# dt and u*dt spread over the partitions through DRAM tiles, so that a state-space scan reads both operands from SBUF

## The chip, the cores and the metric

One NeuronCore of one Trainium2 chip. The metric is the device time of one execution in microseconds (us), the median over runs. Everything is float32.

## The reference

The input is x of shape (2, 2048, 256). Two feed-forward steps stand around a state-space block, each with a residual (layer norms without parameters):

```
x = x + 0.5 * ffn(layernorm(x))      # 8 groups of 512 tokens, W1 (1024x256), W2 (256x1024), no nonlinearity between
x = x + ssm(layernorm(x))
x = x + 0.5 * ffn(layernorm(x))

def ssm(x):                          # 512 inner channels, 16 states each
    x_in, z = split(x @ Wi.T + bi)
    u  = silu(causal depthwise conv of 4 taps over x_in + conv_b)
    dt = softplus(x_in[..., :32] @ Wdt.T + bdt)
    h_t = h_(t-1) * exp(dt_t * A) + dt_t * Bm * u_t          # for every channel and state
    y_t = sum over states of h_t * Cm
    return (y * silu(z)) @ Wo.T + bo + x * Dv.mean()
```

The recurrence over t is the heart: 512 channels x 16 states x 4096 time steps.

## The kernel before, in words

The 4096 tokens go through in four blocks of 1024 (`s` = 0 to 3; blocks 0 and 1 are one sequence, 2 and 3 the other, so the scan state is carried from an even block to the odd one behind it). The 512 channels are cut in eight units of 64 (`j`), two of them to a quarter `q`. For one unit a tile of 128 partitions holds 64 channels x 2 halves of 512 tokens; two of the 32 units, those of quarter 0 in block 0 and quarter 3 in block 3, are laid out otherwise ("wide": 128 channels x 512 tokens, so a scan falls into two of 512 elements).

A scan works on 32 channels x 4 states = 128 partitions and 1024 tokens at once. So each unit takes eight scans: two halves `a` of its channels x four groups `m` of states, in the order that `ORDER` lists. The kernel counts these in one running position `t` from 0 to 255 (8 positions a unit, 64 a block), and all other work is hung on positions.

For a scan (line 691, VectorE, `tensor_tensor_scan`: g = dec * g + v along the tokens) two operands are made:

- `dec` = exp(dt * -A), one ScalarE activation (line 678) from `rep`. `rep` is dt of 32 channels, repeated on the four groups of 32 partitions, by eight DMAs of 64 KB from SBUF to SBUF for each (unit, half) (`spread_dt`, line 646, SyncE's queue). `dec` has four SBUF buffers.
- `v` = u * dt, made by GpSimd (line 630, into a tile `v`) and spread over the partitions by TensorE (`spread_v`, line 662): matmuls with a 0/1 matrix `sel_rep` put it in a PSUM tile of two banks (pool `ps_v`, two buffers, four of the eight PSUM banks). So a scan reads `dec` from SBUF and `v` from PSUM. B and C are folded together into the weights `wy`, which are made once for all 64 columns.

After a scan GpSimd copies its last column to `state` in even blocks (line 693), and TensorE sums over the states (line 700): 16 matmuls (`py`) for each pair of scans, into one PSUM bank (pool `ps_y`, one buffer). ScalarE copies the finished `py` to SBUF (line 707) and GpSimd multiplies it with the gate z (line 711). Everything else in PSUM shares three banks (pool `ps`).

Beside the scans run the preparation of later quarters (`Prepare`: projections on TensorE line 488, the convolution's taps on GpSimd lines 529 and 530, softplus on ScalarE line 94, v on GpSimd line 630), the output projection of the block before (line 732), its second feed-forward step and the first one of the next block (`Ffn`, `Second`: layer-norm sums on VectorE line 322, additions on GpSimd lines 395, 414, 447, 451, 741), and the products W1 W2 of later groups on TensorE (line 259). The first feed-forward step of block 0 and the first operands stand ahead of the loop and are written out by hand.

The order on every engine's queue is the order of the program: nothing reorders it (`manual_schedule`). A table `PL` of positions says at which `t`, counted from the block's or the quarter's start, each step is issued; at one position steps go by kind, those of TensorE behind the others. ScalarE, VectorE, GpSimd and SyncE's DMA queue are in order too, so a step that waits holds up what stands behind it on its own engine. The exponential of scan t is issued three positions ahead (`LA`).

Of the kernel before, what the change touches and what calls it, by code (L numbers as in the profile page):

```python
# [74 lines left out]
def macaron_kernel(ctx: ExitStack, tc: tile.TileContext, x, wi_t, wo_t, wdt_t, par, w1, w2_t, b1, b2, bo, out):  # L75
# [10 lines left out]
    p5 = ctx.enter_context(tc.tile_pool(name="p5", bufs=5))  # L86
    p8 = ctx.enter_context(tc.tile_pool(name="p8", bufs=8))
    ps_y = ctx.enter_context(tc.tile_pool(name="ps_y", bufs=1, space=bass.MemoryType.PSUM))
    ps_v = ctx.enter_context(tc.tile_pool(name="ps_v", bufs=2, space=bass.MemoryType.PSUM))
    ps = ctx.enter_context(tc.tile_pool(name="ps", bufs=3, space=bass.MemoryType.PSUM))  # L90
# [18 lines left out]
    def load_w(g, k, pool=None):  # L109

        w1v = w1[g].rearrange("(p oc) h -> p oc h", p=P)
        w2v = w2_t[g].rearrange("(p oc) h -> p oc h", p=P)
        if pool is None:
            a = wpool.tile([P, NO // 2, DM], F32, tag="w1", name=f"w1_{g}_{k}")
            b = wpool.tile([P, NO // 2, DM], F32, tag="w2", name=f"w2_{g}_{k}")
        else:
            a, b = (
                pool.tile([P, TB], F32, tag="g", name=f"w{i}_{g}_{k}").rearrange("p (a b) -> p a b", b=DM)
                for i in (1, 2)
            )  # L120
        nc.sync.dma_start(a, w1v[:, k * NO // 2 : (k + 1) * NO // 2, :])
        nc.sync.dma_start(b, w2v[:, k * NO // 2 : (k + 1) * NO // 2, :])
        w_sb[g, k] = (a, b)
# [19 lines left out]
    load_w(0, 0)  # L143
    S.dma_start(b1_sb, b1.rearrange("p g o -> p (g o)"))
    load_x(0, 1, S)
    load_w(0, 1)
    for k in range(2):
        load_w(1, k, p5)
    nc.sync.dma_start(wi_sb, wi_t.rearrange("(hh p) d -> p hh d", p=P))

# [44 lines left out]

    early = p2.tile([P, CH], F32, tag="ev", name="early")
    sel32 = early[:, NPAIR * 2 * NM :][:, :32]
    sel_rep = const.tile([P, 2, P], F32, name="sel_rep")
    GP.memset(sel_rep, 0.0)
# [3 lines left out]
    cb_g = early[:, : NPAIR * 2 * NM].rearrange("p (a b) -> p a b", b=1)  # L203
    wy = const.tile([P, NPAIR * 2 * NM, 32], F32, name="wy")
    dv_mean = const.tile([P, 1], F32, name="dv_mean")

    def make_sel_rep():
# [3 lines left out]
        for p in range(4):  # L211
            r = slice(p * 32, (p + 1) * 32)
            GP.tensor_copy(sel_rep[r, p % 2, :].rearrange("p (b c) -> p b c", b=4),
                           sel32[r, :].rearrange("p (b c) -> p b c", b=1).to_broadcast((32, 4, 32)))
# [15 lines left out]
    def make_wy(lo, hi):  # L230
        n = hi - lo
        GP.tensor_tensor(
            wy[:, lo:hi, :], sel32.rearrange("p (a b) -> p a b", a=1).to_broadcast((P, n, 32)),
            cb_g[:, lo:hi, :].to_broadcast((P, n, 32)), ALU.mult,
        )
# [226 lines left out]
    class Prepare:  # L462
# [102 lines left out]
        def exp_table(self, tables=LN_EXP):  # L565
            S.preload_act_table_set(tables)
# [29 lines left out]
        def silu(self):  # L596
            S.activation(self.u, self.u, AF.Silu)  # L597
            self.silu_zs()
# [7 lines left out]
        def start_v(self):  # L606
            v_sb[self.s, self.q] = p1.tile([P, NJ2, CH], F32, tag="v", name=f"v_{self.n}")

        def half_dve(self, u):

            if u == 0:
                self.start_v()
            V.scalar_tensor_tensor(v_sb[self.s, self.q][:, u, :], self.u[:, u, :], 0.5, dts[self.s, self.unit(u)],
                                   ALU.mult, ALU.mult)

        def drive_dve(self, u):
            v = v_sb[self.s, self.q][:, u, :]
            V.scalar_tensor_tensor(v, self.th[:, u, :], 1.0, v, ALU.add, ALU.mult)

        def drive_gp(self, u):  # L620
            if u == 0:
                self.start_v()
            GP.tensor_scalar(self.th[:, u, :], self.th[:, u, :], 0.5, 0.5, ALU.mult, ALU.add)
            GP.tensor_tensor(self.u[:, u, :], self.u[:, u, :], self.th[:, u, :], ALU.mult)
            GP.tensor_tensor(v_sb[self.s, self.q][:, u, :], self.u[:, u, :], dts[self.s, self.unit(u)], ALU.mult)

        def drive(self, eng, u):
            if u == 0:
                self.start_v()
            eng.tensor_tensor(v_sb[self.s, self.q][:, u, :], self.u[:, u, :], dts[self.s, self.unit(u)], ALU.mult)  # L630
# [5 lines left out]
    def column(s, j, a, c, m):  # L636

        group = (j // NJ2) * 4 + (a * 2 + c if is_wide(s, j) else (j % NJ2) * 2 + a)
        return group * NM + m

# [8 lines left out]
    def spread_dt_pe(s, j, a):  # L649

        reps[s, j, a] = []
        for c in range(2):
            t = ps_y.tile([P, CH], F32, tag="py", name=f"pr_{c}") if c else bank(f"pr_{c}")
            r = rows(is_wide(s, j), a, c)
            T.matmul(t, lhsT=sel_rep[r, r.start // 32 % 2, :], rhs=dts[s, j][r, :], start=True, stop=True)
            reps[s, j, a].append(t)

    def spread_v(s, j, a):
        t = ps_v.tile([P, TB], F32, tag="v", name=f"pv_{s}_{j}_{a}")
        for c in range(2):  # L660
            r = rows(True, a, c) if is_wide(s, j) else slice(c * HC, (c + 1) * HC)
            T.matmul(t[:, c * CH : (c + 1) * CH], lhsT=sel_rep[r, c if is_wide(s, j) else a, :],  # L662
                     rhs=v_sb[s, j // NJ2][r, j % NJ2, :], start=True, stop=True)
# [8 lines left out]
    def exponential(t):  # L672
        s, j, a, m = place_of(t)
        decs[t] = p4.tile([P, TB], F32, tag="dec", name=f"dec_{t}")
# [20 lines left out]
    def output(s, j, m):  # L695
        if m == 0:
            pys[s, j] = ps_y.tile([P, CH], F32, tag="py", name=f"py_{s}_{j}")
        for c in range(2):
            for a in range(2):
                T.matmul(pys[s, j][rows(is_wide(s, j), a, c), :], lhsT=wy[:, column(s, j, a, c, m), :],  # L700
# [70 lines left out]
    def fill(n):  # L771

        for _ in range(n):
            T.matmul(next(reversed(pys.values()))[:31, :P], lhsT=b1_pad[:, 0, 1:], rhs=sel_rep[:, 0, :], start=False, stop=False)
# [3 lines left out]
    busy(12)  # L778
    settle(first[0])
    turn(first[0])  # L780
    for hh in range(2):
        combine(0, 0, hh)
    settle(first[1])
    pad_bias(0)
    load_par()
    make_sel_rep()
    bias_pe(0, (0,))
# [3 lines left out]
    bias_pe(0, (1,))  # L791
    bias_act(0)
# [29 lines left out]
    begin.exp_table(EXP)  # L822
# [12 lines left out]
    make_wy(0, 16)  # L835
# [9 lines left out]
    PL = {'g0': 8, 'g1': 11, 'si': 12, 'po0': 3, 'po1': 7, 'poa': 4, 'c0': 12, 'c1': 28, 'f3a': 13, 'f3b': 17, 'f1a': 20, 'f1b': 30, 'sa': 32, 'sb': 41, 'nw': 0, 'nr': 2, 'tp0': 3, 'ta0': 5, 'tp1': 4, 'ta1': 6, 'bi': 7, 'pr0': 7, 'pr1': 8, 'ad0': 9, 'ad1': 10, 'rs': 3, 'rb': 7, 'i0': 0, 'i1': 0, 'ia': 2, 'ed': 2, 'ce': 3, 'tp': 5, 'dr': 12, 'dv0': 4, 'dv1': 7, 'cb': 8, 'bp': 2, 'ba': 5, 'sp': 8, 'sq': 9, 'lw': 6, 'lx0': 16, 'lx1': 28, 'st': 12, 'r0': 0, 'r1': 4, 'xg0': 2, 'xs0': 5, 'xf0': 7, 'xf1': 16, 'xg1': 8, 'xs1': 14, 'xw': 23, 'xp0': 12, 'xp1': 29, 'xd': 18, 'xr0': 29, 'xb0': 35, 'xr1': 32, 'xb1': 40, 'y0': 11, 'y1': 12, 'y2': 13, 'y3': 17, 'y4': 16, 'y5': 18, 'z0': 6, 'z1': 8, 'z2': 8, 'z3': 10, 'ga': 2, 'gm': 2, 'eo': 3, 'en': 4, 'ep': 6, 'eb': 8, 'u0': 1, 'u1': 1, 'u2': 1, 'u3': 2, 'u4': 3, 'u5': 4, 'u6': 5, 'u7': 5, 'u8': 6, 'u9': 7, 'ua': 11}  # L845
    plan = {}

    def at(t, fn, *a, name=None):
# [4 lines left out]
        if t % 1:  # L853
            kind = 4
# [9 lines left out]
    def put_ffn(t, s, h, name):  # L864
        put(t, lambda: Ffn(s, h, name), (0, "stats"), (PL["nw"], "newton", GP), (PL["nr"], "normalise", 0, GP),
            (PL["nr"], "normalise", 1, GP), (PL["tp0"], "turn_pe", 0), (PL["ta0"], "turn_act", 0),
            (PL["tp1"], "turn_pe", 1), (PL["ta1"], "turn_act", 1), (PL["bi"], "bias", GP), (PL["pr0"], "product", 0),
            (PL["pr1"], "product", 1), (PL["ad0"], "add_act", 0), (PL["ad0"], "add_gp", 0),
            (PL["ad1"], "add_act", 1), (PL["ad1"], "add_gp", 1))

    def put_second(t, s, h):
        put(t, lambda: Second(s, h), (0, "stats"), (PL["nw"], "newton", GP), (PL["nr"], "normalise", 0, GP),
            (PL["nr"], "normalise", 1, GP), (PL["tp0"], "turn_pe", 0), (PL["ta0"], "turn_act", 0),
            (PL["tp1"], "turn_pe", 1), (PL["ta1"], "turn_act", 1), (PL["rs"], "residual"), (PL["rb"], "residual_bias"))

    def put_prepare(t, s, q):
        if (s, q) == (0, 1):
# [3 lines left out]
                (PL["z3"], "drive_gp", 0),  # L881
# [3 lines left out]
        steps = [(PL["i0"], "inner_pe", 0), (PL["i1"], "inner_pe", 1), (PL["ia"], "start_xi"), (PL["ia"], "inner_act", 0),  # L885
                 (PL["ia"], "inner_act", 1), (PL["ed"], "edges"), (PL["ce"], "centre", 0), (PL["ce"], "centre", 1)]
        steps += [(PL["tp"] + n, "tap", k, i)
                  for n, (k, i) in enumerate((k, i) for k in (2, 1, 0) for i in range(NJ2))]
        steps += [(PL["g0"], "gate_pe", 0), (PL["g1"], "gate_pe", 1), (PL["si"], "silu"),
                  (PL["dr"], "drive", GP, 0), (PL["dr"], "drive", GP, 1)]  # L890
        if q == 0:
            for j in range(NPAIR):
                d = PL["dv0"] if j < NPAIR // 2 else PL["dv1"]
                steps += [(d, "dt_pe", j), (d, "dt_act", j)] + ([(d, "exp_table")] if j % 4 == 3 else [])
        put(t, lambda: Prepare(s, q), *steps)
# [3 lines left out]
    for t, method, *a in (  # L899
# [7 lines left out]
        (PL["u6"], begin.dt_pe, 1), (PL["u6"], begin.dt_act, 1), (PL["u6"], begin.exp_table, EXP),  # L907
# [4 lines left out]
        (PL["ua"] + 0.5, begin.exp_table, EXP),  # L912
        (PL["xg1"], begin.gate_pe, 1), (PL["xs1"], begin.gate_z, 1), (PL["xs1"], begin.gate_z_times, 1),
        (13, make_wy, 16, 32), (PL["xw"], make_wy, 32, 64),
# [6 lines left out]
    for s in range(NB):  # L921
        b = s * PER
        for j in range(NPAIR):
            t = b + j * NPOS
            nxt = (s, j + 1) if j + 1 < NPAIR else (s + 1, 0)
            if nxt[0] < NB:
                for k in range(2):
                    at({(0, 1): 6, (0, 2): 10}.get(nxt, t + PL[f"r{k}"]), spread_dt, *nxt, k)
# [3 lines left out]
        for q in range(NQ):  # L932
            if q + 1 < NQ:
                put_prepare(b + q * 2 * NPOS, s, q + 1)
            elif s + 1 < NB:
                put_prepare(b + q * 2 * NPOS, s + 1, 0)
# [152 lines left out]
```

## Time and profile before

| | |
|---|---|
| median of two runs | 767.4 us (766.62 and 768.19) |
| the profiled execution | 764.32 us, span in the trace 762.5 us |
| granted TensorE clock in it, mean | 0.937 |
| busy, share of the span: TensorE | 642.3 us, 84% |
| VectorE | 638.6 us, 84%, of it the scans 574.4 us |
| ScalarE | 527.1 us, 69%, of it the exponentials dec 292.4 us |
| GpSimd | 512.9 us, 67% |
| DMA of SyncE's queue | 59.84 MB, 28.9% of 16 DMA engines |

Busy time is time in which an instruction ran; the idle time of an engine is listed with what ended it (its releaser). The first scan starts at 42.2 us and the last ends about 744 us, so the span falls into a head of 42 us, the scans with all that runs beside them, and a tail of 18.5 us.

### The profile page before, as it was taken

What the parts mean: (1) busy time and instruction counts of PE and PEld (TensorE: products, weight loads), DVE (VectorE), ACT (ScalarE), POOL (GpSimd) and SP (SyncE); (2) the same over time, 40 slices, a digit from 0 to 9 for tenths busy, and PEclk for the clock granted to TensorE, in tenths of its full rate; (3) what the DMA queues carried; (4) which work ended last, traced back from release to release, by engine and by line L of the source; (5) the groups of instructions that cost most, each with busy time, mean ns of one, the idle gap of its engine ahead of it and who ended that gap; (6) DMA issues with size and microseconds to landing.
All of it is one profiled execution on the core that took longest, in us unless ns stands there. A gap on an engine that the chain in (4) does not pass through costs nothing.

```text
span 762.5 us, 10406 instructions
## 1 busy us (share of the span) xinstructions
PE 642.3 (84%) x3428; PEld 277.1 (36%) x3428; DVE 638.6 (84%) x553; ACT 527.1 (69%) x658; POOL 512.9 (67%) x821
## 2 busy tenths in 40 slices
PE   9999795993879998897888998897697989677966
PEld 7634241440212543542211643353121524212534
DVE  3587777793999989776999989776999999999995
ACT  3467885753899576765899675757699777768631
POOL 5125658899854759979853779989964678753321
PEclk9999799997899999999899999999799999897989
DMA  8274216242122325415122325313122222322101
GB/s 298 72 220 113 55 29 166 56 125 68 28 56 65 74 56 155 135 38 160 40 55 56 73 67 142 112 51 75 37 56 55 56 57 75 92 56 55 29 1 55
DMA packets 42789, 62.29 MB, mean 82 GB/s; under 512 B 12536, under 2 KB 22128, under 8 KB 42736
## 3 DMA queue, kind: packets, MB, share of 16 engines
q1 hardware_dynamic: 41344, 59.84, 28.9%
q0 software_dynamic: 720, 1.24, 0.6%
q8 instruction: 27, 0.44, 0.2%
q10 hardware_dynamic: 672, 0.56, 0.2%
q14 instruction: 26, 0.21, 0.1%
HBM read 24.08 MB, written 4.19 MB: 37 GB/s over the span
## 4 chain that ended last, share of the span: by engine, by line
PE 39%; POOL 22%; DVE 13%; ACT 11%; issue 6%; DMA 6%; SPq 2%; ACTq 0%; DVEq 0%; POOLq 0%
DVE g L691 11%; PE pwc L259 7%; PE py L700 7%; PE po L732 7%; POOL u L530 5%; ACT dec L678 5%; PE pv L662 4%; DMA rep<-dt 3%; PE pf_f L402 3%; PE pxi L488 3%; POOL tap L529 3%; DMA w<-in_w_t 2%; POOL x L414 2%; POOL x L395 2%; PE pz L488 2%
## 5 line engine op out<-in xcount | busy, mean ns | idle before, releaser
L678 ACT ACTIVATE dec<-rep,neg_a 128x1024 f32<-128x1024 f32 (+1 forms) x280 | 287.6, 1059 | 122.4 <-DVE g L691 82.9
L691 DVE TENSOR_TENSOR_SCAN g<-dec,state,pv 128x1024 f32<-128x1024 f32 (+1 forms) x160 | 309.5, 2003 | 26.6 <-PE py L700 13.0
L691 DVE TENSOR_TENSOR_SCAN g<-dec,pv 128x1024 f32<-128x1024 f32 (+1 forms) x128 | 264.9, 2131 | 34.4 <-PE py L700 17.2
L700 PE MATMUL py<-g,wy 128*32 128x512 f32 x1024 | 167.7, 654 | 51.1 <-ACT ev_y L707 35.0
L530 POOL TENSOR_TENSOR u<-u,tap 128x512 f32<-128x512 f32 x90 | 114.2, 1268 | 9.0 <-ACT u L524 1.6
L662 PE MATMUL pv<-v,sel_rep 64*128 64x512 f32 (+1 forms) x256 | 72.8, 663 | 31.9 <-POOL v L630 15.2
L693 POOL COPY state<-g 128x1 f32<-128x1 f32 x160 | 27.5, 185 | 80.0 <-DVE g L691 80.0
L700 PEld LDWEIGHTS py<-g,wy 128*32 128x32 f32 x1024 | 25.2, 111 | 147.4 <-issue 60.6
L711 POOL TENSOR_TENSOR z<-ev_y,z 128x512 f32<-128x512 f32 x31 | 39.6, 1276 | 50.3 <-ACT ev_y L707 50.3
L402 PE MATMUL pf_f<-wc,xnt_f 128*128 128x256 f32 x256 | 66.5, 405 | 5.9 <-ACT ev_f L410 4.3
L529 POOL TENSOR_SCALAR tap<-xi,par_p 128x512 f32<-128x512 f32 x84 | 58.1, 692 | 8.7 <-DMA xi<-xi 5.4
L488 PE MATMUL pz<-xn2t,wi_sb 128*64 128x512 f32 x224 | 61.9, 681 | 0.0
L259 PE MATMUL pwc<-w,w 128*128 128x256 f32 x256 | 60.8, 386 | 0.2 <-ACT dt L94 0.2
L402 PEld LDWEIGHTS pf_f<-wc,xnt_f 128*128 128x128 f32 x256 | 48.0, 197 | 32.5 <-ACT ev_f L410 8.2
L732 PE MATMUL po<-wo_sb,z 64*128 64x256 f32 x448 | 54.6, 391 | 0.8 <-POOL z L711 0.7
L259 PEld LDWEIGHTS pwc<-w,w 128*128 128x128 f32 x256 | 47.1, 190 | 18.4 <-issue 8.9
L488 PE MATMUL pxi<-xn2t,wi_sb 128*64 128x512 f32 x224 | 51.1, 598 | 0.0
L732 PEld LDWEIGHTS po<-wo_sb,z 64*128 64x128 f32 x448 | 43.5, 192 | 16.8 <-issue 10.6
L395 POOL TENSOR_TENSOR x<-x,bc 128x1024 f32<-128x1024 f32 x14 | 33.0, 2355 | 23.4 <-ACT xn_f L361 23.4
L662 PEld LDWEIGHTS pv<-v,sel_rep 64*128 64x128 f32 (+1 forms) x256 | 19.6, 190 | 75.6 <-DVE g L691 35.3
L630 POOL TENSOR_TENSOR v<-u,dt 128x512 f32<-128x512 f32 x28 | 35.0, 1270 | 6.9 <-ACT u L597 6.9
L414 POOL TENSOR_TENSOR x<-ev_f,x 128x512 f32<-128x512 f32 x24 | 30.4, 1269 | 3.1 <-ACT ev_f L410 3.1
(158 smaller groups left out, 745.1 us busy)
## 6 DMA issues: line engine op xcount, KB each, us to landing
rep<-dt SPq DMA_DIRECT2D x496, 64.0 KB, 2.0
w<-in_w SPq DMA_DIRECT2D x16, 512.0 KB, 6.9
w<-in_w_t SPq DMA_DIRECT2D x16, 512.0 KB, 8.7
x<-in_x SPq DMA_DIRECT2D x7, 512.0 KB, 3.9
out<-x SPq DMA_DIRECT2D x6, 512.0 KB, 3.2
wi_sb<-in_wi_t SPq DMA_DIRECT2D x1, 1024.0 KB, 13.8
wo_sb<-in_wo_t SPq DMA_DIRECT2D x2, 512.0 KB, 6.7
out<-x SPq DMA_DIRECT2D x4, 256.0 KB, 2.2
```

Source lines behind the costliest of these rows:

```text
L259: T.matmul(pt, lhsT=a[:, oc, hh * P : (hh + 1) * P], rhs=b[:, oc, :], start=(k == 0 and oc == 0), stop=(k == 1 and oc == NO // 2 - 1),)
L395: eng.tensor_tensor(self.xs, self.xs, bc[self.g].to_broadcast((P, GT, DM)), ALU.add)
L402: T.matmul(o, lhsT=self.xt[pair][:, hh, k * P : (k + 1) * P], rhs=wc[self.g][:, hh, :], start=(hh == 0), stop=(hh == NH - 1 and not bias))
L414: GP.tensor_tensor(part, self.ev.rearrange("p (a b) -> p a b", a=2), part, ALU.add)
L488: T.matmul(pt[h * HC : (h + 1) * HC, :], lhsT=wi_sb[:, hh, k : k + HC], rhs=xn2t[self.s, h][:, hh, :], start=(hh == 0), stop=(hh == NH - 1))
L529: GP.tensor_scalar(tap, self.xi[:, u, k : k + CH], self.par(C_CW, NK, u, k), 0.0, ALU.mult, ALU.add)
L530: GP.tensor_tensor(self.u[:, u, :], self.u[:, u, :], tap, ALU.add)
L662: T.matmul(t[:, c * CH : (c + 1) * CH], lhsT=sel_rep[r, c if is_wide(s, j) else a, :], rhs=v_sb[s, j // NJ2][r, j % NJ2, :], start=True, s ...
L678: S.activation(decs[t][:, c * w : (c + 1) * w], part, AF.Exp, scale=neg_a[:, i : i + 1])
L691: V.tensor_tensor_scan(g[:, r], dec[:, r], v[:, r], 0.0 if first else state[:, i : i + 1], ALU.mult, ALU.add)
L700: T.matmul(pys[s, j][rows(is_wide(s, j), a, c), :], lhsT=wy[:, column(s, j, a, c, m), :], rhs=gs[a, m][:, c * CH : (c + 1) * CH], start=(m ...
L732: T.matmul(held_po[s, pair][h][:, k * DM : (k + 1) * DM], lhsT=lhsT, rhs=rhs, start=((q, i) == parts[0]), stop=((q, i) == parts[-1]))
```

## The change

- `dt` and `v` of each unit are written to DRAM tiles of 128 x 512 by one DMA (`to_dram`) and read back into SBUF four times, once for each group of 32 partitions (`from_dram`: four DMAs of 128 KB for each half, for dt into `rep`, for v into a new tile `vr` with three buffers). All go through SyncE's queue. Units 0 and 1 of block 0 keep the old ways: `spread_dt`, and `spread_v` by TensorE, whose second half ScalarE copies to SBUF.
- `v` is written in place of u; the tile `v` is gone. `wy` is made anew for each quarter (16 columns, two buffers; 16 GpSimd instructions of 512 elements where there were three, two of 512 and one of 1024).
- PSUM: `ps_y` two buffers for one, `ps_v` one (of two banks) for two, `ps` four banks for three. From position 16 on every fourth `dec` (t % 4 == 3) lies in the `ps_v` tile; the others have three SBUF buffers.
- For quarter 0 of blocks 1 to 3 the first half of u's silu is made as a tanh on ScalarE and two GpSimd instructions (`gate_ev`, `drive_gp`). The table set EXP is loaded in place of LN_EXP behind most preparations.
- Two weight DMAs at the start go to ScalarE's queue, the head's order is changed a little, and `PL` gets positions for each block's and each quarter's step, with an order within a position. A group's weights are loaded in four parts at positions of their own.

The numbers of SyncE's DMAs go from 576 to 634: 480 of `rep<-dt` become 240 reads of dt, and 240 reads of v and 60 writes are new.

```diff
-    ps_y = ctx.enter_context(tc.tile_pool(name="ps_y", bufs=1, space=bass.MemoryType.PSUM))
-    ps_v = ctx.enter_context(tc.tile_pool(name="ps_v", bufs=2, space=bass.MemoryType.PSUM))
-    ps = ctx.enter_context(tc.tile_pool(name="ps", bufs=3, space=bass.MemoryType.PSUM))
+    pv = ctx.enter_context(tc.tile_pool(name="pv", bufs=3))
+    ps_y = ctx.enter_context(tc.tile_pool(name="ps_y", bufs=2, space=bass.MemoryType.PSUM))
+    ps_v = ctx.enter_context(tc.tile_pool(name="ps_v", bufs=1, space=bass.MemoryType.PSUM))
+    ps = ctx.enter_context(tc.tile_pool(name="ps", bufs=4, space=bass.MemoryType.PSUM))
+    dram = ctx.enter_context(tc.tile_pool(name="dram", bufs=16, space=bass.MemoryType.DRAM))
...
-    def make_wy(lo, hi):
-        n = hi - lo
+    def make_wy(q):
+        n = 4 * NM
+        wy[q] = p2.tile([P, n, 32], F32, tag="wy", name=f"wy_{q}")
         GP.tensor_tensor(
...
+        def gate_ev(self):
+            self.th = p2.tile([P, 1, CH], F32, tag="ev", name=f"th_{self.n}")
+            S.activation(self.th[:, 0, :], self.u[:, 0, :], AF.Tanh, scale=0.5)
...
         def drive(self, eng, u):
-            if u == 0:
-                self.start_v()
-            eng.tensor_tensor(v_sb[self.s, self.q][:, u, :], self.u[:, u, :], dts[self.s, self.unit(u)], ALU.mult)
+            v_sb[self.s, self.unit(u)] = self.u[:, u, :]
+            eng.tensor_tensor(self.u[:, u, :], self.u[:, u, :], dts[self.s, self.unit(u)], ALU.mult)
+
+        def v_out(self, u):
+            v_d[self.s, self.unit(u)] = to_dram(v_sb[self.s, self.unit(u)], "vd")
+
+        def dt_out(self, j):
+            dt_d[self.s, j] = to_dram(dts[self.s, j], "dtd")
...
+    def to_dram(t, tag):
+        d = dram.tile([P, CH], F32, tag=tag, name=f"{tag}_{len(v_d)}_{len(dt_d)}")
+        nc.sync.dma_start(d, t)
+        return d
+
+    def from_dram(t, d, s, j, a):
+        part = d.rearrange("(a c p) t -> a p c t" if is_wide(s, j) else "(c a p) t -> a p c t", a=2, c=2)[a]
+        for n in range(4):
+            nc.sync.dma_start(t[n * 32 : (n + 1) * 32, :].rearrange("p (c t) -> p c t", c=2), part)
+
+    def spread_dt_dram(s, j, a):
+        t = p3.tile([P, TB], F32, tag="rep", name=f"rep_{s}_{j}_{a}")
+        from_dram(t, dt_d[s, j], s, j, a)
...
+    def spread_v_dram(s, j, a):
+        vs[s, j, a] = pv.tile([P, TB], F32, tag="vr", name=f"vr_{s}_{j}_{a}")
+        from_dram(vs[s, j, a], v_d[s, j], s, j, a)
...
     def exponential(t):
         s, j, a, m = place_of(t)
-        decs[t] = p4.tile([P, TB], F32, tag="dec", name=f"dec_{t}")
+        decs[t] = (ps_v.tile([P, TB], F32, tag="v", name=f"dec_{t}") if t % 4 == 3 and t >= 2 * NPOS else
+                   p3.tile([P, TB], F32, tag="dec", name=f"dec_{t}"))
...
-                    at({(0, 1): 6, (0, 2): 10}.get(nxt, t + PL[f"r{k}"]), spread_dt, *nxt, k)
+                    if nxt == (0, 1):
+                        at(6, spread_dt, *nxt, k)
+                    else:
+                        at(10 if nxt == (0, 2) else t + PL[f"r{k}"], spread_dt_dram, *nxt, k)
+                        at(t + PL[f"rv{k}"], spread_v_dram, *nxt, k)
...
-        if pos in (5, 7) and t + NPOS - pos < end and t != 5:
-            ns, nj = divmod(t // NPOS + 1, NPAIR)
-            for a in (0, 1) if t == 7 else (k,):
-                spread_v(ns, nj, a)
+        if t == 7:
+            for a in range(2):
+                spread_v(0, 1, a)
```

The reads of dt for the next unit are issued at its predecessor's positions 0 and 4 (`r0`, `r1`), those of v at 4 and 6 (`rv0`, `rv1`).

## The prediction, made before the changed kernel was run

> **What bounds the kernel now.** I read the page's busy line first, then the busy time by stage (head, scans, tail), then the groups of instructions, and last the waits. The busy line, and the three stages (columns: stretch, its length, busy us of PE, PEld, DVE, ACT, POOL with instruction counts, granted clock, DMA share, GB/s):
>
> ```profile
> PE 642.3 (84%) x3428; PEld 277.1 (36%) x3428; DVE 638.6 (84%) x553; ACT 527.1 (69%) x658; POOL 512.9 (67%) x821
> ```
> ```profile
> 0.00:42.20 42.20, 40.28 (x215) 27.06 (x216) 17.47 (x67) 18.18 (x34) 13.84 (x43) 1.00 0.54 177
> 42.20:744.00 701.80, 589.53 (x3154) 241.30 (x3158) 611.77 (x464) 506.74 (x620) 496.70 (x777) 0.93 0.29 77
> 744.00:762.50 18.50, 12.47 (x64) 8.73 (x60) 9.34 (x23) 2.18 (x5) 2.35 (x1) 0.97 0.16 57
> ```
>
> The 701.8 us between head and tail decide. VectorE works 611.8 of them, so 90.0 us are to be had there at most as long as VectorE's work stays. GpSimd works 496.7 and has 205.1 idle: the change has to leave it that slack. The groups that matter:
>
> ```profile
> L691 DVE TENSOR_TENSOR_SCAN g<-dec,state,pv 128x1024 f32<-128x1024 f32 x112 | 252.5, 2322 | 17.2 <-PE py L700 11.1 <-ACT dec L678 3.2 <-PE pv L662 2.8
> L691 DVE TENSOR_TENSOR_SCAN g<-dec,pv 128x1024 f32<-128x1024 f32 x112 | 246.7, 2265 | 32.1 <-PE py L700 17.2 <-POOL tap L529 4.0 <-POOL state L693 3.5
> ```
> ```profile
> L530 POOL TENSOR_TENSOR u<-u,tap 128x512 f32<-128x512 f32 x90 | 114.2, 1268 | 9.0 <-ACT u L524 1.6
> L395 POOL TENSOR_TENSOR x<-x,bc 128x1024 f32<-128x1024 f32 x14 | 33.0, 2355 | 23.4 <-ACT xn_f L361 23.4
> ```
>
> The waits (total us, times, longest) say why VectorE idles: TensorE gives `g` buffers back late, and TensorE is late because its one `py` bank is not yet emptied.
>
> ```profile
> ACT dec L678 <- DMA rep<-dt: 38.4, 8, 8.6
> PE py L700 <- ACT ev_y L707: 35.0, 14, 6.3
> DVE g L691 <- PE py L700: 30.2, 18, 2.8
> DVE st_l L322 <- POOL x L414: 22.5, 6, 5.9
> DVE g L691 <- PE pv L662: 7.7, 3, 2.8
> ```
>
> **What is new beside what.** Today a steady scan reads one tensor in SBUF (`dec`) and one in PSUM (`pv`). GpSimd's instructions do not notice it: v = u * dt, all 28, lies between 1257 and 1288 ns. The only VectorE instructions with two SBUF tensors of 512 elements (u at L533, v at L613 and L618) lie in the head and between 61 and 68 us, where GpSimd has nothing to read (by the timeline it idles from 61.7 to 65.3 us, around three of the six u, and then issues DMAs):
>
> ```profile
> L630 POOL TENSOR_TENSOR v<-u,dt x28: 1257/1270/1288, 139.7 to 695.7; 128x512 f32<-128x512 f32 x28
> ```
> ```profile
> L533 DVE SCALAR_TENSOR_TENSOR u<-xi,par_w,u x6: 751/752/753, 35.4 to 63.4; 128x512 f32<-128x512 f32 x6
> ```
>
> So the trace shows no scan with two SBUF tensors beside a reading GpSimd, and after the change these two are the steady state. Counted over the 256 positions: from 16 on three in four (180) have `dec` and `vr` both in SBUF, and eight before that; 188 in all. In the other 68 one operand is in PSUM.
>
> **The change part by part**, against the profiled execution (span 762.5, time 764.3, so 1.8 us around the span; the median 767.4 is 0.4% above it).
>
> 1. TensorE loses 120 of the 128 spreads of v. Its row has 256 records for 72.8 us, so 240 x 0.284 = 68.3 us go; it falls from 642 to about 574. With two `py` banks its 35.0 us of waiting for ev_y mostly go as well. On VectorE this is worth at most 30.2 + 7.7 = 37.9 us and at least nothing; I take 32, as TensorE has both causes lifted. Of the 22.5 us for x at L414 the new places may save some: nothing to 22.5, I take 8. Late next is then VectorE itself, or GpSimd.
> 2. The scan's own duration: a VectorE instruction of 512 elements takes 684 ns with a PSUM operand (x at L418) and 680 to 692 without (v at L613 and L618). I take no change; bounds minus and plus 10 ns x 188 = 2 us.
> 3. GpSimd: 16 `wy` of 512 at 1.044 us for 4.0 us of the three old ones, +12.7; three tanh paths of 0.62 + 1.27, +5.7. In the middle 496.7 becomes 515, of which about 5 (DMA issues, memsets) read nothing. This hides in 205 us of idle, if the next point leaves them.
> 4. The collision, if there is one. Low end: nothing, the nearest row by neighbour (scans with one SBUF tensor). High end: a two-tensor scan and a reading GpSimd instruction never run together. In between lies a row-made price: GpSimd's two-input instruction grows from 1268 to 2355 ns for 512 elements more, that is 1024 reads, 1.06 ns a read; it reads its two inputs one after the other. If VectorE's second stream joins that queue, a scan brings 1024 reads, 1.09 us, and 188 scans 205 us, to be added to GpSimd's 515: 720 us. I take this value: it is the only one made from what a second stream from SBUF costs in this trace.
> 5. ScalarE: 3 tanh, 4 copies (0.58) and two weight DMAs more, 5 us; `dec` to PSUM for one in four. It has 195 us of idle in the middle. Cost 0.
> 6. SyncE: 634 DMAs for 576, at a median issue of 0.59 us: 374 us for 340, of 762. A unit's reads are issued at its predecessor's positions 0 to 6, four or more positions (9 us) before use; four issues of 0.59 and a landing of 2.0 (today's 64 KB) to 3.9 us (512 KB from DRAM) make 4.4 to 6.3 us, hidden. The write ahead of it (2.2 us, as out<-x of 256 KB) is issued when GpSimd has made v; SyncE then stands in that wait, and the dt reads, x, weights and edge DMAs behind it wait too. Today SyncE waits 150.6 us for xi at L511 without harm except the 38.4 us at `dec`. Cost between 0 and 2 us for each of 30 units; I take 0 where GpSimd is the bound, since there the write is late with GpSimd anyway. Traffic: 59.8 MB on this queue plus 31 MB of v read and 60 x 0.26 MB written, about 107, so 29% of the DMA engines becomes some 52%.
> 7. Head and tail: the same work in another order, 60.7 us kept (plus or minus 3).
>
> **The sum.** VectorE alone would need 701.8 - 32 - 8 = 662 us for the middle. GpSimd needs 720, and 10 more for waits it can't avoid (of 205 today). So GpSimd is the bound: 42.2 + 730 + 18.5 + 1.8 = **792 us**.
>
> [...] The row for point 4 is that GpSimd's v takes 1257 to 1288 ns beside scans with one SBUF tensor. [...] The row for point 2 is 684 ns with PSUM against 680 to 692 without. [...]
>
> **The rivals.**
> - No collision (faster): the mechanism is that the second stream costs GpSimd nothing. Then VectorE bounds: 42.2 + 662 + 18.5 + 1.8 = **724**. For it: all 28 v within 31 ns today. Against: that row has only one SBUF tensor. It decides as long as a scan takes less than (662 - 515) / 188 = 0.78 us from GpSimd. Range 705 to 750.
> - Exclusion (much slower): 168 scans of 2.229 us and 20 wide positions of 2.35 are 421 us in which GpSimd reads nothing, then its 510: the middle is 931 and the time **994**. For it: GpSimd's reads come one after the other, so its way to SBUF is narrow. Against: nothing in the trace shows an engine stopped so. Range 950 to 1030.
> - Late operands: no collision, but v's way through DRAM arrives 1 to 2 us late for each of 30 units. 724 + 45 = **769**. For it: 38.4 us of `dec` waiting for `rep` today, landings of up to 9.4 us. Against: 9 us of lead, and these waits were eight.
>
> **How the numbers follow.** Sharing, my forecast, 0.36 (its own range 770 to 830); no collision 0.28; exclusion 0.28; late operands 0.06; the rest 0.02. The three prices of point 4 hang on something no row shows, so the range has to span them: from 715 (about 0.07 lies below) to 1010 (about 0.09 above). A measurement of this kernel tells about 2% from no change, 752 to 783. Faster: 0.26 of no collision, 0.03 of sharing, 0.01 of late: 0.30. Same: 0.02 + 0.09 + 0.03 = 0.14. Slower: the rest, 0.56.
>
> **What would show it.** Point 4: GpSimd's two-input row at 1268 ns grows to 1.6 to 2 us and its busy share to over 90%: sharing; rows that scatter by whole scans, or scans of 3 us and more: exclusion; 1268 unchanged: no collision, and VectorE's busy share near 90%. Point 1: `pv` gone down to 16 records, the wait for ev_y under 10 us. Point 2: scans at 2.26 to 2.32 us. Point 6: waits of scans for `vr` over 20 us would mean late operands. The forecast is wrong if GpSimd's rows don't change, or if they lengthen by a whole scan each.

## The result, and the profile after

| | before | after |
|---|---|---|
| median of two runs | 767.4 us | 1024.0 us (1022.99 and 1025.09) |
| profiled span | 762.5 us | 1021.2 us |
| granted TensorE clock, mean | 0.937 | 0.801 |
| VectorE busy | 638.6 us | 719.2 us |
| GpSimd busy | 512.9 us | 851.5 us |
| DMA of SyncE's queue | 59.84 MB | 105.98 MB, 37.3% of 16 engines |

The ratio after to before is 1.334, 95% interval 1.326 to 1.343: the change makes the kernel a third slower. The forecast of 792 us was too low, and 1024 lies above its range; the rival "exclusion" had 994 (950 to 1030), near the measured time, but by two errors that cancel (see point 4 below).

The busy line of after, and its three stages (columns as in the prediction: stretch, length, busy us of PE, PEld, DVE, ACT, POOL, granted clock, DMA share, GB/s):

```profile
PE 657.5 (64%) x3176; PEld 285.5 (28%) x3176; DVE 719.2 (70%) x553; ACT 527.1 (52%) x665; POOL 851.5 (83%) x838
```
```profile
0.00:45.00 45.00, 38.16 (x184) 26.39 (x186) 16.52 (x66) 14.65 (x27) 12.96 (x41) 0.96 0.48 158
45.00:1000.00 955.00, 603.99 (x2922) 247.61 (x2918) 693.39 (x465) 510.24 (x634) 836.21 (x796) 0.79 0.39 106
1000.00:1021.20 21.20, 15.32 (x73) 11.45 (x72) 9.33 (x23) 2.18 (x5) 2.35 (x1) 0.98 0.14 51
```

All of the loss is in the middle. VectorE now stands idle there for 262 us, and GpSimd, with 836 of 955 us, is the busiest engine. GpSimd was given some 18 us of new work (the prediction's estimate, point 3) and is busy 340 us more. Its groups and those of the scans show where (line, engine, operation, out<-in, shape, count, busy, mean ns, idle before and its releasers):

```profile
L536 POOL TENSOR_TENSOR u<-u,tap 128x512 f32<-128x512 f32 x90 | 169.9, 1887 | 7.5
L535 POOL TENSOR_SCALAR tap<-xi,par_p 128x512 f32<-128x512 f32 x84 | 117.2, 1395 | 22.9 <-DMA xi<-xi 17.0 <-ACT dec L718 3.9
L733 POOL COPY state<-g 128x1 f32<-128x1 f32 x160 | 74.8, 485 | 37.7 <-DVE g L731 36.5
```
```profile
L731 DVE TENSOR_TENSOR_SCAN g<-dec,state,vr 128x1024 f32<-128x1024 f32 x112 | 289.1, 2641 | 68.8 <-PE py L740 42.7 <-ACT dec L718 19.1 <-issue 6.5
L731 DVE TENSOR_TENSOR_SCAN g<-dec,vr 128x1024 f32<-128x1024 f32 x112 | 280.9, 2555 | 106.5 <-ACT dec L718 34.8 <-PE py L740 34.4 <-POOL state L733 30.6
```

The tap addition went from 1268 ns to 1887 on the mean, and the scans from 2322 and 2265 to 2641 and 2555. Both sides pay: VectorE is busy 82 us more in the middle, GpSimd, its new work set aside, some 320, four times as much. A mean hides how, so look at single instructions. The timeline of after around 410 us (start us, duration us, engine and line; "x2" are two instructions in one row):

```profile
408.63 2.35 DVE L731 TENSOR_TENSOR_SCAN g<-dec,state,vr 128x1024 f32<-128x1024 f32 x1 [3.90 <-ACT dec L718]
408.75 3.29 POOL L536 TENSOR_TENSOR u<-u,tap 128x512 f32<-128x512 f32 x1
412.00 1.26 POOL L420 TENSOR_TENSOR x<-ev_f,x 128x512 f32<-128x512 f32 x1
...
415.53 2.53 POOL L634 TENSOR_TENSOR u<-u,dt 128x512 f32<-128x512 f32 x2
...
416.88 6.53 DVE L731 TENSOR_TENSOR_SCAN g<-dec,state,vr 128x1024 f32<-128x1024 f32 x2 [5.89 <-PE py L740]
...
418.02 3.25 POOL L420 TENSOR_TENSOR x<-ev_f,x 128x512 f32<-128x512 f32 x1
...
421.23 3.25 POOL L751 TENSOR_TENSOR z<-ev_y,z 128x512 f32<-128x512 f32 x1
424.44 1.27 POOL L420 TENSOR_TENSOR x<-ev_f,x 128x512 f32<-128x512 f32 x1
```

The tap addition of 408.75 starts 0.12 us behind a scan and ends 1.06 us after it: it stood through nearly the whole scan and then did its 1.26 us (the two overlap by 0.2). At 412.00, with VectorE idle, the same kind of instruction takes 1.26. The two scans from 416.88 take 3.27 us each: each first waits about 1 us for a GpSimd instruction that is under way (the second of the two of 415.53, then that of 418.02). That is the sign that the prediction gave for exclusion: rows that lengthen by whole scans, scans of 3 us.

### The profile page after: what moved, and what is told of

Read it like the earlier page. It is cut to its first block, busy times and chain, and to the rows that moved or that the text cites. A ratio compares the mean times of both kernels' runs of the same rounds, so it can differ in the third digit from the quotient of the medians.

```text
span 1021.2 us, 10053 instructions
## 1 busy us (share of the span) xinstructions
PE 657.5 (64%) x3176; PEld 285.5 (28%) x3176; DVE 719.2 (70%) x553; ACT 527.1 (52%) x665; POOL 851.5 (83%) x838
## 3 DMA queue, kind: packets, MB, share of 16 engines
q1 hardware_dynamic: 65056, 105.98, 37.3%
## 5 line engine op out<-in xcount | busy, mean ns | idle before, releaser
L731 DVE TENSOR_TENSOR_SCAN g<-dec,state,vr 128x1024 f32<-128x1024 f32 (+1 forms) x152 | 344.9, 2331 | 73.3 <-PE py L740 44.5
L731 DVE TENSOR_TENSOR_SCAN g<-dec,vr 128x1024 f32<-128x1024 f32 (+1 forms) x120 | 290.0, 2464 | 106.5 <-ACT dec L718 34.8
L740 PE MATMUL py<-g,wy 128*32 128x512 f32 x1024 | 199.9, 715 | 125.9 <-DVE g L731 125.8
L536 POOL TENSOR_TENSOR u<-u,tap 128x512 f32<-128x512 f32 x90 | 169.9, 1887 | 7.5
L535 POOL TENSOR_SCALAR tap<-xi,par_p 128x512 f32<-128x512 f32 x84 | 117.2, 1395 | 22.9 <-DMA xi<-xi 17.0
L733 POOL COPY state<-g 128x1 f32<-128x1 f32 x160 | 74.8, 485 | 37.7 <-DVE g L731 36.5
L376 PE MATMUL ptr_f<-ident,xn_f 128*128 128x128 f32 x128 | 28.3, 351 | 75.8 <-POOL xn_f L369 69.6
L751 POOL TENSOR_TENSOR z<-ev_y,z 128x512 f32<-128x512 f32 x31 | 55.4, 1788 | 20.6 <-ACT ev_y L747 20.6
L376 PE MATMUL ptr_l<-ident,xn_l 128*128 128x128 f32 x64 | 17.4, 390 | 76.4 <-POOL xn_l L369 75.9
L607 ACT ACTIVATE u<-u 128x1024 f32<-128x1024 f32 (+1 forms) x14 | 13.5, 965 | 96.9 <-POOL u L536 96.9
L772 PE MATMUL po<-wo_sb,z 64*128 64x256 f32 x448 | 57.2, 410 | 3.5 <-POOL z L751 3.5
L328 DVE BATCH_NORM_STATS2 st_f<-x 128x6 f32<-128x256 f32 x64 | 22.6, 407 | 41.5 <-POOL x L781 26.5
```

The costliest lines, as they stand in the source:

```text
L535: GP.tensor_scalar(tap, self.xi[:, u, k : k + CH], self.par(C_CW, NK, u, k), 0.0, ALU.mult, ALU.add)
L536: GP.tensor_tensor(self.u[:, u, :], self.u[:, u, :], tap, ALU.add)
L731: V.tensor_tensor_scan(g[:, r], dec[:, r], v[:, r], 0.0 if first else state[:, i : i + 1], ALU.mult, ALU.add)
L733: GP.tensor_copy(state[:, i : i + 1], g[:, (c + 1) * w - 1 : (c + 1) * w])
L740: T.matmul(pys[s, j][rows(is_wide(s, j), a, c), :], lhsT=wy[j // NJ2][:, column(s, j, a, c, m) % (4 * NM), :], rhs=gs[a, m][:, c * CH : (c ...
L751: GP.tensor_tensor(z, held_ev.pop((s, j)), z, ALU.mult)
```

## The experiments

Eleven kernels were run. Medians are beside a median of the kernel before from the same chip; the ratio in brackets is to that kernel before, with its 95% interval. The kernel after has its two runs of above alone, beside 767.4. The theories: **exclusion** (a scan with two SBUF tensors and a reading GpSimd instruction do not run together), **sharing** (the forecast: a scan takes 1.09 us of reads from GpSimd), and, for the loss of 257 us, something else in the change: the way through DRAM, PSUM or the order.

**1. The pair by itself.** A kernel that does nothing of the reference: stages of 12 scans on VectorE (128 x 1024) beside 20 or 40 independent GpSimd instructions, with the operands' places changed from stage to stage.

> The kernel leaves out the whole computation; its output is zeros. In eleven stages, parted by small copies that wait on both engines, it runs twelve scans of 1024 on VectorE, alone or beside GpSimd instructions, with the scan's second operand in PSUM or in SBUF. Exclusion (a VectorE instruction with two SBUF tensors and a GpSimd instruction that reads SBUF never run together): beside two-SBUF scans a GpSimd two-input instruction of 512 (1.27 us alone) and a scan (2.27 us alone) take their sum, so the stage of 12 scans and 20 GpSimd instructions lasts 27 + 25 = 52 us; with one scan operand in PSUM, whichever one, it lasts 27 us and both rows are as alone; one-input GpSimd instructions are held too, memsets are not. Sharing by element: the same stage lasts some 27 to 40 us and the GpSimd row is 1.6 to 2 us, without whole-scan steps. No collision: 27 us everywhere.

Duration of single instructions, min / median / max in ns:

| VectorE's scan reads | beside GpSimd's | scan | GpSimd |
|---|---|---|---|
| SBUF and PSUM | nothing | 2263 (mean) | |
| two from SBUF | nothing | 2268 (mean) | |
| nothing | two-input, 128 x 512 | | 1262 (mean) |
| SBUF and PSUM | two-input | 2262 (mean) | 1260 / 1276 / 1300 |
| PSUM (`dec`) and SBUF (`v`) | two-input | 2267 (mean) | 1256 / 1259 / 1267 |
| two from SBUF | two-input | 2267 / 3280 / 3285 | 1255 / 3238 / 3302 |
| two from SBUF | one-input, 128 x 512 (617 alone) | 2266 / 2625 / 2632 | 612 / 2579 / 2650 |
| two from SBUF | copies of 128 x 1 | 2264 / 2267 / 2281 | 179 / 183 / 2245 |
| two from SBUF | memset, 128 x 512 | 2268 (mean) | 519 (mean) |

The row of the pair in that trace (columns: count, min/median/max ns, first and last start):

```profile
L80 DVE TENSOR_TENSOR_SCAN g<-dec_s,v_s x12: 2267/3280/3285, 126.0 to 159.2; 128x1024 f32<-128x1024 f32 x12
```
```profile
L82 POOL TENSOR_TENSOR r<-a_s,b_s x20: 1255/3238/3302, 128.3 to 173.3; 128x512 f32<-128x512 f32 x20
```

One tensor in PSUM, whichever of the two, and there is no collision here: GpSimd's two-input instruction takes 1276 and 1259 ns at the median, 1262 alone. With both in SBUF the engines go by turns: one GpSimd instruction gets in behind each scan, and each waits for the other (3238 and 3280 ns). It is nearly a sum: 3.28 us for the pair where the two alone take 2.27 + 1.26 = 3.53; the stage lasts 48.5 us, where exclusion had said 52 and no collision 27. Even a copy of one column stands up to a whole scan long (2245 ns at the longest, 183 at the median). The memset, which reads nothing, does not wait: 519 ns beside the scans, 525 and 524 for the two of its shape ahead of the first scan. Sharing by reads has fallen here: the one-input instruction brings half the reads and waits as long (2579 - 617 = 1962 ns, against 3238 - 1262 = 1976).

**2 and 3. The kernel after with and without the collision.** The two kernels differ in one expression, the memory in which `dec` lies (and with it the number of its buffers, two in PSUM and three in SBUF); both are the kernel after with the PSUM split of before, most steps at their old positions, and `dec` made two positions ahead. The edit that tells them apart, first kernel:

```diff
-        decs[t] = (ps_v.tile([P, TB], F32, tag="v", name=f"dec_{t}") if t % 4 == 3 and t >= 2 * NPOS else
+        decs[t] = (ps_v.tile([P, TB], F32, tag="v", name=f"dec_{t}") if t >= 2 * NPOS else
                    p3.tile([P, TB], F32, tag="dec", name=f"dec_{t}"))
```

In the second kernel the condition is `if False`, so that all of `dec` lies in SBUF.

> The changed kernel with every dec from position 16 on in PSUM (two buffers, issued two positions ahead and behind the position's other steps; one py bank and three shared banks, most steps put at the places that they had before the change). v and dt still go through DRAM. No scan from position 16 on has two SBUF tensors. Exclusion: GpSimd's rows go back to 1.27 us, scans to 2.3 us, and the time falls from 1024 to between 720 and 800 (VectorE's 612 us in the middle bind, ScalarE's two dec buffers may cost some). If the way through DRAM, its late operands or SyncE's longer queue had made the time, it would stay above 950.

> The same kernel as c_psum in its order, pools and DMAs, but every dec in SBUF (three buffers): the only difference is where dec lies. All but eight of the 256 positions then have two SBUF tensors (248; the changed kernel has 188). Exclusion: 248 x 2.235 + 510 of GpSimd reads + 62 for head and tail = 1126, and some waits above it: 1100 to 1200. Sharing at 1.09 us a scan: 515 + 270 + 62 = 847. DRAM or queue as the cause: within 3% of c_psum.

Measured: 867.4 us with `dec` in PSUM (ratio 1.130, 1.126 to 1.134), 1152.8 with `dec` in SBUF (1.502, 1.496 to 1.508). The tap addition in the one and in the other:

```profile
L536 POOL TENSOR_TENSOR u<-u,tap 128x512 f32<-128x512 f32 x90 | 116.3, 1293 | 7.5
```
```profile
L536 POOL TENSOR_TENSOR u<-u,tap 128x512 f32<-128x512 f32 x90 | 160.6, 1785 | 7.5
```

285 us hang on where one operand lies, and the kernel with fewer buffers for it is the faster. The second lies where exclusion had put it (1100 to 1200; sharing had 847, DRAM or the queue 3% from the first). The first missed the expected 720 to 800: even without the collision it is 100 us slower than before. Its waits point to what took the collision's place, ScalarE and VectorE handing two PSUM buffers to and fro, and the single `py` bank (no run takes the two apart):

```profile
ACT dec L718 <- DVE g L731: 147.7, 131, 5.4
...
PE py L740 <- ACT ev_y L747: 90.5, 21, 11.0
...
DVE g L731 <- ACT dec L718: 82.2, 19, 11.1
```

Before, these waits were 82.9, 35.0 and 12.8 us. So this way out of the collision, as tried, doesn't pay.

The middle of the two gives more: the same 796 GpSimd instructions, with 8 two-SBUF positions in the first, 188 in after and 248 in the second (the stretch of each, as above):

```profile
45.00:845.00 800.00, 581.78 (x2930) 238.39 (x2926) 617.54 (x464) 517.49 (x634) 522.69 (x796) 0.86 0.47 127
```
```profile
45.00:1130.00 1085.00, 645.15 (x2927) 253.80 (x2924) 700.14 (x463) 515.47 (x634) 934.14 (x796) 0.75 0.34 93
```

GpSimd's busy time is 522.7, 836.2 and 934.1 us: (836.2 - 522.7) / 180 = 1.74 us more for each two-SBUF position, and (934.1 - 836.2) / 60 = 1.63 for each further one; between the first and the second, which differ in `dec` alone, it is (934.1 - 522.7) / 240 = 1.71. That fits a price for each scan. (A position of a wide quarter holds two scans of 512. The two wide quarters are four units, not two, and 20 of the 188 positions are such.)

**4 and 5. TensorE's relief by itself.** The kernel before without the spreads of v (later units scan the first unit's v), and the same with the PSUM split of after.

```diff
-        if pos in (5, 7) and t + NPOS - pos < end and t != 5:
+        if pos == 7 and t + 1 < end:
...
-                spread_v(ns, nj, a)
+                vs[ns, nj, a] = vs[0, 0, a]
```

> The kernel before, with its scans from PSUM, but every unit from the second on scans the v tiles of the first unit, which stay in PSUM: 126 of the 128 spread groups on TensorE are left out, so the scan inputs of all later units are not theirs. It isolates point 1 of the prediction, the relief of TensorE, with no VectorE instruction that reads two SBUF tensors in the loop. If point 1 holds (up to 30.2 + 7.7 us of VectorE's waits for TensorE, with one py bank still in place): 730 to 750 us. If the waits for py are set by the one bank and ScalarE's emptying of it: 755 to 765. In both, GpSimd's u row stays at 1.26 to 1.29 us and the scans at 2.26 to 2.33.

> As the run with the spreads left out, and PSUM shared out as in the kernel after: two py banks, four banks for the rest, one v tile that both halves scan. Again the scan inputs of later units are not theirs. It is the most that TensorE's relief and the banks can bring with scans from PSUM. Point 1 as forecast: 764 - 32 = about 732 us (725 to 740), TensorE's wait for ev_y under 10 us. If TensorE's lateness was not what VectorE's waits came from, 750 to 765.

Measured: 749.2 us (0.976, 0.970 to 0.982) and 744.7 (0.971, 0.964 to 0.978), against 765.7. So what the change was to gain is there: 21 us with both, two thirds of the 32 that point 1 gave to TensorE's relief (its other 8, for new places of the steps, these runs don't try). The second kernel missed its expected 725 to 740. TensorE's wait for ev_y (35.0 us before) is 41.2 in the first kernel and gone from the second, so it took the second bank. The waits of VectorE in the second kernel show where the rest went:

```profile
DVE st_l L322 <- POOL x L414: 30.7, 7, 8.6
DVE g L691 <- ACT dec L678: 12.4, 8, 3.3
DVE st_f L322 <- DMA x<-in_x: 12.3, 4, 5.0
DVE g L691 <- PE py L700: 12.1, 8, 3.9
```

Scans wait for `py` 12.1 us instead of 30.2 and no more for `pv` (7.7 before); but the wait for x grew from 22.5 to 30.7.

**6 and 7. Does GpSimd pay for each instruction?** Experiment 1 suggested that it is the number of GpSimd instructions that counts, since each waited for a scan. Two kernels test that on the kernel after: the 160 state copies moved to VectorE, and each tap addition split in two halves.

```diff
-                GP.tensor_copy(state[:, i : i + 1], g[:, (c + 1) * w - 1 : (c + 1) * w])
+                V.tensor_copy(state[:, i : i + 1], g[:, (c + 1) * w - 1 : (c + 1) * w])
```
```diff
-            GP.tensor_tensor(self.u[:, u, :], self.u[:, u, :], tap, ALU.add)
+            for c in range(2):
+                r = slice(c * DM, (c + 1) * DM)
+                GP.tensor_tensor(self.u[:, u, r], self.u[:, u, r], tap[:, r], ALU.add)
```

> The kernel after with one edit: the 160 copies of the last column to state (128 x 1) move from GpSimd to VectorE. Theory of turns (beside a scan with two SBUF tensors GpSimd gets one reading instruction through for each scan and waits about 2 us for it, whatever its length; 160 x 0.485 = 74.8 us of rows): GpSimd loses 160 instructions, of which about half fall beside such scans; 75 to 110 us are saved, VectorE pays 160 x about 0.1 = 16 to 24 us where it isn't waiting anyway: 925 to 965 us. Theory of bandwidth (what a GpSimd instruction suffers goes by what it reads; a copy of 128 elements in all reads next to nothing): GpSimd saves about 20 us, VectorE loses as much: 1005 to 1030 us.

> The kernel after with one edit: each tap addition on GpSimd (u, 128 x 512, 90 of them) is made as two of 128 x 256, the same reads and writes in twice as many instructions. Theory of turns: 90 instructions more, each of which waits some 2 us if it stands beside a two-SBUF scan (about three in four of them in three quarters of the time), against the half length saved: 90 to 180 us more, 1100 to 1200 us. Theory of bandwidth: only the fixed cost of 90 instructions more, about 0.16 us each: 14 us, 1030 to 1045 us.

Measured: 1011.2 us (1009.96 to 1013.87) and 1047.9 (1046.61 to 1048.66), that is 13 less and 24 more than 1024.0 (ratios 1.318 and 1.365 for 1.334). The theory of turns, a price for each GpSimd instruction, has fallen. The theory of bandwidth had 1005 to 1030 and 1030 to 1045, so these two times do not speak against it; experiment 1 does, where a copy of 128 x 1 took up to 2.2 us. The waiting only changes its owner: without the state copies some other rows are longer (z 2142 ns instead of 1788, the tap addition 2016 instead of 1887),

```profile
L751 POOL TENSOR_TENSOR z<-ev_y,z 128x512 f32<-128x512 f32 x31 | 66.4, 2142 | 32.5 <-ACT ev_y L747 30.8 <-DMA rep<-dtd 1.6
```

and GpSimd's busy time in the middle falls by 836.2 - 797.1 = 39 us, little more than the copies' own 160 x 0.19 = 30. After the split it rises by 853.4 - 836.2 = 17 us, near the 526.6 - 512.9 = 13.7 that the same split adds in the kernel before (experiment 8; the two stretches, the state copies moved and the tap additions split):

```profile
45.00:990.00 945.00, 605.42 (x2923) 245.03 (x2923) 723.26 (x625) 511.73 (x635) 797.07 (x636) 0.79 0.39 107
```
```profile
45.00:1020.00 975.00, 606.35 (x2921) 250.34 (x2919) 675.94 (x463) 511.61 (x635) 853.41 (x886) 0.78 0.38 104
```

With 160 instructions fewer or 90 more, GpSimd's time beyond its own work hardly moves. So what counts is the number of scans: each stops GpSimd about once, whatever stands there.

**8. The split in the kernel before**, as a control.

> The control to the split tap additions: the same split in the kernel before, 90 GpSimd instructions more, about 14 us of fixed cost. GpSimd has idle time there, so within 5 us of 766 us by every theory.

771.4 us against 768.3 (1.004, 1.002 to 1.006). The 90 more instructions cost 3 us where GpSimd has idle time and 24 in the kernel after, where it has little.

**9 and 10. Is GpSimd's own work on the path?** The two bias additions are left out, in after and, as a control, in before.

```diff
-            eng.tensor_tensor(self.xs, self.xs, bc[self.g].to_broadcast((P, GT, DM)), ALU.add)
+            pass
...
-            GP.tensor_tensor(self.xs, self.xs, bo_all.to_broadcast((P, GT, DM)), ALU.add)
+            pass
```

> The kernel after without the two bias additions on GpSimd (L401, 14 of 128 x 1024, and L457, 8 of 128 x 1024), so the biases are missing from the result. In the kernel before these two take 33.0 + 18.9 = 51.9 us undisturbed, in the kernel after 68.1. Theory that times add (while a two-SBUF scan runs GpSimd reads nothing, so the stage lasts as long as those scans and GpSimd's own work together): 52 us are saved, 972 us (960 to 985). Theory of a price per instruction: 22 instructions, at most 22 us for their turns, and their own time hidden: 1000 to 1024. If the bound is a chain elsewhere (ScalarE, TensorE): 1010 to 1024.

> The control: the kernel before without the same two additions (L395, L451), 51.9 us of GpSimd's work less. GpSimd has 205 us of idle in the middle, so little follows: 755 to 767 us, a few us from x coming earlier to the statistics at L322 (22.5 us of waiting).

Measured: 983.3 us in after's form (982.7 to 985.11), 41 less than 1024.0; and 752.4 against 768.3 in before's (0.980, 0.977 to 0.984), 16 less. Of 52 us of GpSimd's work, 41 come back in the kernel after, within the 960 to 985 of the theory that times add: its work is on the path there, at four fifths of its price. The control gained 16 and missed its 755 to 767, so part of this work was on the path before too, through x and the statistics (22.5 us of waiting before, 12.2 here). What the kernel after adds to that is 25 us.

**11. The way through DRAM by itself.** The kernel before with dt, and only dt, written to DRAM and read back.

```diff
+            if (self.s, j) not in ((0, 0), (0, 1)):
+                dt_d[self.s, j] = to_dram(dts[self.s, j], "dtd")
...
-                    at({(0, 1): 6, (0, 2): 10}.get(nxt, t + PL[f"r{k}"]), spread_dt, *nxt, k)
+                    at({(0, 1): 6, (0, 2): 10}.get(nxt, t + PL[f"r{k}"]), spread_dt if nxt == (0, 1) else spread_dt_dram, *nxt, k)
```

> One part of the change alone: the kernel before with dt, and only dt, written to DRAM and read back four times for each half (from unit 2 on); v is still spread by TensorE into PSUM, so every scan has one operand in PSUM. If the way through DRAM is harmless (point 6): 755 to 768 us, as some of the 38.4 us that ScalarE waits for rep may go. If it makes dec late (late operands): 775 to 790. By every theory of the collision GpSimd's u row stays at 1.27 us.

765.2 us against 768.3 (0.995, 0.993 to 0.997). This part does no harm, and ScalarE's wait for the reads from DRAM is 25.8 us where that for `rep` was 38.4 (another 5.0 are waits for `rep` of the units that keep the old way). It is the only kernel with the whole computation that is faster than before, by half a per cent. The way of v through DRAM wasn't run alone.

## Why the prediction was wrong, point by point

The direction (slower 0.56) and the place were right: GpSimd became the bound, by the collision of two-SBUF scans with its reads. The step that failed is the value taken in point 4, 1.09 us a scan from a queue of reads, where the runs show 1.74 us of standing still; and behind it the term of the sum "10 more for waits it can't avoid", where GpSimd was idle for 119 us.

1. TensorE's relief: right in kind, too large. 21 us of 32 (experiments 4 and 5); the 8 for x were not tried. In after the wait for ev_y is gone too, as forecast, but no time is gained by it: VectorE isn't the bound, and it waits 79.0 us for `py` where it waited 30.2. TensorE's busy time did not fall either: 657.5 us for 642.3 with 16 records of `pv` left, at a lower granted clock (0.79 in the middle for 0.93), where a `py` matmul takes 715 ns for 654.
2. The scan's own duration: right, 2268 ns with two SBUF tensors and 2263 with one in PSUM (experiment 1).
3. GpSimd's own work, 515 us: right. 522.7 less 8 x 1.74 is 509.
4. The collision: 1.09 us a scan was taken, 1.74 was measured (after against experiment 2): 188 x 1.74 = 327 us for 205. The price was built from the number of reads. GpSimd's own time about doubles with the second input (617 and 1262 ns), its waiting does not grow with it (1962 and 1976 ns, experiment 1). The rival's price, the whole scan of 2.24 us in which GpSimd stands (421 us), was too high: the pair overlaps by 0.25 us, and GpSimd may at times have had no instruction waiting when a scan began (not counted). The rival's 994 came near 1024 by luck: it had 94 us too much for the scans and nothing for the 119 us of idle time. The prediction's ground against exclusion, that no engine is seen stopped so, was no evidence: in the trace of before no instruction could have shown it. Experiment 1 shows it: 3238 ns for GpSimd's 1262 beside two SBUF tensors, 1276 beside one, and 519 for the memset, which only writes.
5. ScalarE: busy 527.1 us in both, as forecast. That the cost was 0 isn't shown: VectorE waits 57.2 us for `dec` in after, 12.8 before, and no run takes apart whether the places in PSUM, ScalarE's order or GpSimd's lateness made these waits.
6. The way through DRAM: right. Reads land 2.9 and 3.1 us after issue on the median, scans wait for `vr` 0.2 us in the whole run (over 20 was the sign), `dec` waits 22.9 us for DMAs where it waited 38.4, and experiment 11 has dt's part alone at 0.995. "Late operands" is refuted.
7. Head and tail: 45 + 21.2 = 66.2 us between the cuts shown, for 60.7 (plus or minus 3). The first scan starts at 48.3 us, 6 later than before; why wasn't looked into.

The sum for the middle was 515 + 205 + 10 = 730. Measured: 509 of own work, 327 stopped by scans, and 119 idle (955 - 836.2), 955 together. So the collision's size accounts for 122 us of the miss and the idle time for 109; own work takes 6 back, and head and tail add 5.5. 792 + 122 + 109 - 6 + 5.5 = 1022.5, against the 1023.0 of the profiled execution (span 1021.2 and 1.8).

The 10 us had no row behind them. 24 of the 119 lie in the first 45 us of the stretch, where the first scans run and GpSimd has little to do (21.0 us of work from 45 to 90); before, GpSimd was idle there for 19 us (42.2 to 75) too. From 90 us to 1000 it is idle for 95 us; what ended that (the four longest in total):

```profile
POOL z L751 <- ACT ev_y L747: 20.6, 7, 6.3
POOL tap L535 <- DMA xi<-xi: 17.0, 3, 7.6
POOL state L733 <- DVE g L731: 9.9, 5, 4.4
POOL x L401 <- ACT xn_f L367: 9.0, 1, 9.0
```

Only 9.9 us are a direct wait for a scan; two larger ones come through ScalarE and a DMA, and some 30 us stand in no row of this list. On the other side VectorE, idle for 262 us, waits in after for:

```profile
DVE g L731 <- PE py L740: 79.0, 19, 7.4
DVE g L731 <- ACT dec L718: 57.2, 12, 8.6
DVE st_l L328 <- POOL x L420: 41.4, 12, 9.9
DVE g L731 <- POOL state L733: 33.9, 15, 4.4
```

Two of these four name GpSimd. Behind the `py` and `dec` waits it may stand too (ScalarE waited 96.9 us for u from L536, and 27.5 in `ev_y` for x from L781, with `py` held). That the two engines wait for each other in this way, VectorE for what GpSimd is late with and GpSimd for what then comes late, is read from these waits; no run tests it, and the cause of the 119 us stays open.

A kernel that keeps the relief without the collision was not found. Putting all of `dec` in PSUM is 100 us slower than before (experiment 2), and the 21 us of experiment 5 need the spreads gone.

## What to carry to other kernels

Before moving a VectorE operand from PSUM to SBUF, ask whether the other one is in SBUF too and what GpSimd does meanwhile: here one PSUM operand kept the engines apart (1276 ns for GpSimd's 1262), and two SBUF operands made them take turns (3238). Price it as (number of such VectorE instructions) x (most of their duration, here 1.74 of 2.24 us), added to GpSimd's own work; if that sum passes the time of the stage before, GpSimd bounds the kernel, and more idle time may come on top (119 us here). Splitting GpSimd's instructions, or giving some away, then did little (24 us more, 13 less). A relief on one engine is worth at most what the bounding engine waits for it in the trace (37.9 us), and here a little more than half of that, as the next wait grew.

## What was not expected of the hardware

- The turns were one for one in experiment 1: with both queues full, 11 or 12 GpSimd instructions started beside 12 scans, were they of 0.18 us (128 x 1) or of 1.26 (by the rows' means, 40 x (749 - 183) / 2062 and 20 x (2350 - 1262) / 1976, 11 each). The copy of 128 x 1 didn't delay the scan (2267 ns), the two-input instruction delayed it by 1.0 us (3280) and the one-input by 0.36 (2625).
- A plain two-input VectorE instruction (128 x 1024) collided as the scan did: 1210 ns at the shortest and 2278 at the median, beside GpSimd's 2239 on the mean.
- TensorE's granted clock was 0.86, 0.79 and 0.75 in the middles of the kernels with 8, 188 and 248 two-SBUF positions, where TensorE was busy 73%, 63% and 59% of the time. No run shows that the one follows from the other; in the tail of after it was busy 72% at a clock of 0.98.
